# A planned instruction order, and the recurrent state brought back through DVE squares and DRAM, in a four-layer graph network on one core

## The chip, the core and the metric

The kernel runs on one core of a Trainium2 chip. The metric is the time of one execution on the device, in microseconds (us); less is better. Each ratio below compares a kernel with the kernel before, run on the same chip, one after the other. The experiments ran on three chips, and on each the kernel before came out within 0.6 us of the others in its median, so medians are compared across them too.

Engines: PE is TensorE (matmuls and transposes), PEld its weight loads, DVE the vector engine, ACT the scalar engine, POOL GpSimd, SP the engine that issues most of the DMAs here. PE multiplies a stationary operand (the weights, 128x128) with a moving one (up to 512 columns).

## The reference, cut to what matters

```python
x: (32, 512, 128)   adj: (512, 512)          # 32 batches of 512 tokens with 128 features
x = x + gcn(relu(layernorm(x)))              # A_norm @ h @ W.T + b
x = x + ggnn(relu(layernorm(x)))             # five recurrent steps, below
x = x + elu(gat(relu(layernorm(x))))         # attention over the edges
x = x + gat(relu(layernorm(x)))

def step(h):                                 # of ggnn, five times
    m = adj @ h
    av = concat([m, m])
    u3 = h @ u3_w.T + u3_b
    z = sigmoid(av @ w3_w.T + w3_b + u3)
    r = sigmoid(av @ w4_w.T + w4_b + u3)
    hv = tanh(av @ w5_w.T + w5_b + (r * h) @ u5_w.T + u5_b)
    return (1 - z) * h + z * hv
```

All of it is float32. The batches are independent, the five steps of a batch are not.

## The kernel before

In a step, `adj @ h` needs the state with tokens on the partitions (`h`, it is the stationary operand), everything after it needs the features on the partitions (`hT`). Four batches ("lanes") are in flight, one step apart, so that PE always has another batch's work. After each step PE transposes the new `hT` back:

```python
def product(p, h, mT):
    for c in range(C):                                        # C = 4 chunks of 128 tokens
        nc.tensor.matmul(flat(p), h[:, c, :], mT[:, c, :], start=(c == 0), stop=(c == C - 1))

def ggnn_reset(b, s):
    ...
    nc.tensor.matmul(flat(p), wT["w4"], m, start=True, stop=False)
    nc.tensor.matmul(flat(p), wT["u3"], hT, start=False, stop=True)
    nc.scalar.activation(r, flat(p), AF.Tanh, bias=gate_b["w4"], scale=0.5)
    nc.vector.scalar_tensor_tensor(rh, r, 1.0, hT, op0=ALU.add, op1=ALU.mult)

def ggnn_update(b, s):
    ...                                                       # z the same way with w3
    nc.tensor.matmul(flat(q), wT["w5"], m, start=True, stop=False)
    nc.tensor.matmul(flat(q), wT["u5"], rh, start=False, stop=True)     # PE needs rh here
    nc.scalar.activation(hv, flat(q), AF.Tanh, bias=gate_b["w5"])
    ...                                                       # three DVE operations make the new hT

def ggnn_back(b, s):
    p = bank("back")
    to_features(p, hT.rearrange("p (c k) -> p c k", c=C))     # four PE transposes
    if s < STEPS - 1:
        h = work.tile([P, C, D], F32, name="h", bufs=LANES + 3)
        nc.scalar.copy(flat(h), flat(p))
    else:
        nc.vector.scalar_tensor_tensor(flat(xs[b]), flat(xs[b]), -1.0, flat(p), ...)

def gat_edges(b, l):                                          # four of these stand on DVE per layer
    for j in range(C):
        nc.vector.scalar_tensor_tensor(e[:, j, :], flat(row), h[:, j, D + 1:D + 2], maskT[l][:, j, :],
                                       op0=ALU.max, op1=ALU.mult)

def wide():                                                   # one double PSUM bank for all GAT layers
    return psum.tile([P, C, 2 * P], F32, name="wide")
```

The functions are called in a fixed pattern of turns. From that the framework's own scheduler makes the order in which each engine takes its instructions.

The softmax here doesn't subtract the row's maximum and nothing guards it: scores larger than these inputs give would overflow.

Of the kernel before, what the change touches and what calls it, by code (L numbers as in the profile page):

```python
# [16 lines left out]
SLOPE = 0.2  # L17
LANES = 4


@with_exitstack
def gnn_stack(ctx: ExitStack, tc: tile.TileContext, a: dict, out: bass.AP):
# [5 lines left out]
    const = ctx.enter_context(tc.tile_pool(name="const", bufs=1))  # L28
    state = ctx.enter_context(tc.tile_pool(name="state", bufs=1))
    stat = ctx.enter_context(tc.tile_pool(name="stat", bufs=4))  # L30

    psum = ctx.enter_context(tc.tile_pool(name="psum", bufs=1, space=bass.MemoryType.PSUM))

    def bank(name, bufs=1):
        return psum.tile([P, C, P], F32, name=name, bufs=bufs)

    def side_bank():
        return bank("side", 2)

    def wide():  # L40
        return psum.tile([P, C, 2 * P], F32, name="wide")
# [3 lines left out]


    setup = ctx.enter_context(ExitStack())
    raw = setup.enter_context(tc.tile_pool(name="raw", bufs=1))
    adj_sb = raw.tile([P, C, N], F32, name="adj_sb")
    for c in range(C):  # L50
        nc.sync.dma_start(adj_sb[:, c, :], adj[c * P:(c + 1) * P, :])

    def load(pool, name, shape, src):
        t = pool.tile(shape, F32, name=name)
        nc.scalar.dma_start(t, src)
        return t

    def column(v):
        return v if len(v.shape) == 2 else v.rearrange("(p o) -> p o", o=1)

    w0 = load(raw, "w0", [P, D], a["L0_gnn_W"])
    b0 = load(const, "b0", [P, D], bass.AP(tensor=a["L0_gnn_b"].tensor, offset=a["L0_gnn_b"].offset,
                                           ap=[[0, P], [1, D]]))
    w1 = {k: load(raw, k, [P, a["L1_gnn_" + k + "_w"].shape[1]], a["L1_gnn_" + k + "_w"])
          for k in ("w3", "u3", "w4", "w5", "u5")}
    b1 = {k: load(raw, "b" + k, [P, 1], column(a["L1_gnn_" + k + "_b"]))
          for k in ("w3", "u3", "w4", "w5", "u5")}
    gat_w = {2: a["L2_gnn_W"], 3: a["L3_gnn_w"]}
    w_aug, a_pair = {}, {}
    for l in (2, 3):  # L70
        w_aug[l] = const.tile([P, D + 3], F32, name=f"w_aug{l}")
        nc.scalar.dma_start(w_aug[l][:, :D], gat_w[l])
        a_pair[l] = raw.tile([P, 2], F32, name=f"a_pair{l}")
        nc.scalar.dma_start(a_pair[l][:, 0:1], column(a[f"L{l}_gnn_a_src"]))
        nc.scalar.dma_start(a_pair[l][:, 1:2], column(a[f"L{l}_gnn_a_dst"]))

    xs = []
    for b in range(B):
        t = state.tile([P, C, D], F32, name=f"x{b}")
        nc.sync.dma_start(t, x[b].rearrange("(c p) d -> p c d", p=P))  # L80
        xs.append(t)


    ident = const.tile([P, P], F32, name="ident")
    make_identity(nc, ident)
    mhalf = const.tile([P, C], F32, name="mhalf")
    nc.gpsimd.memset(mhalf, -0.5)

    adjT = const.tile([P, C, N], F32, name="adjT")
    for m in range(C):  # L90
        p = side_bank()
        for c in range(C):
            nc.tensor.transpose(p[:, c, :], adj_sb[:, c, m * P:(m + 1) * P], ident)
        nc.scalar.copy(adjT[:, m, :], flat(p))
    deg = raw.tile([P, C], F32, name="deg")
    nc.vector.reduce_sum(deg, adj_sb, axis=mybir.AxisListType.X)
    nc.vector.tensor_scalar_add(deg, deg, 1.0)
    dinv = raw.tile([P, C], F32, name="dinv")
    nc.gpsimd.tensor_tensor(dinv, deg, mhalf, ALU.pow)


    anT = const.tile([P, C, N], F32, name="anT")
    nc.vector.tensor_copy(anT, adjT)
    for c in range(C):
        blk = anT[:, c, c * P:(c + 1) * P]
        nc.vector.tensor_add(blk, blk, ident)
    drow = side_bank()
    for c in range(C):
        nc.tensor.transpose(drow[:, c, :], dinv[:, c:c + 1].to_broadcast([P, P]), ident)
    maskT = {l: const.tile([P, C, N], BF16, name=f"maskT{l}") for l in (2, 3)}  # L110
    nc.vector.tensor_scalar(maskT[2], anT, 0.0, None, op0=ALU.is_gt)
    for m in range(C):
        nc.vector.scalar_tensor_tensor(anT[:, m, :], anT[:, m, :], dinv[:, m:m + 1], flat(drow),
                                       op0=ALU.mult, op1=ALU.mult)
    nc.vector.tensor_scalar(maskT[3], adjT, 0.0, None, op0=ALU.is_gt)

    def transposed(name, w, scale=None):
        p = side_bank()
        nc.tensor.transpose(p[:, 0, :], w, ident)
        t = const.tile([P, P], F32, name=name)  # L120
        if scale is None:
            nc.scalar.copy(t, p[:, 0, :])
        else:
            nc.scalar.mul(t, p[:, 0, :], scale)
        return t

    w0T = transposed("w0T", w0)


    ws = {}  # L130
    for k in ("w3", "w4", "w5"):
        ws[k] = raw.tile([P, D], F32, name=k + "s")
        nc.vector.tensor_add(ws[k], w1[k][:, :D], w1[k][:, D:])
    nc.vector.tensor_sub(ws["w3"], ws["w3"], ws["w4"])
    wT = {k: transposed(k + "T", ws[k]) for k in ("w4", "w3", "w5")}
    wT["u3"] = transposed("u3T", w1["u3"])
    wT["u5"] = transposed("u5T", w1["u5"], 0.5)
    gate_b = {}
    for k, u, half in (("w3", "u3", True), ("w4", "u3", True), ("w5", "u5", False)):
        gate_b[k] = const.tile([P, 1], F32, name="gate_b" + k)  # L140
        nc.vector.tensor_add(gate_b[k], b1[k], b1[u])
        if half:
            nc.vector.tensor_scalar_mul(gate_b[k], gate_b[k], 0.5)


    for l in (2, 3):
        gT = transposed(f"gat_wT{l}", w_aug[l][:, :D])
        a3 = raw.tile([P, 3], F32, name=f"a3_{l}")
        nc.vector.tensor_scalar_mul(a3[:, 0:1], a_pair[l][:, 1:2], SLOPE)
        nc.vector.tensor_scalar_mul(a3[:, 1:2], a_pair[l][:, 1:2], 1.0 - SLOPE)  # L150
        nc.vector.tensor_scalar_mul(a3[:, 2:3], a_pair[l][:, 0:1], SLOPE - 1.0)
        p = side_bank()
        nc.tensor.matmul(p[:, 0, :3], gT, a3, start=True, stop=True)
        nc.vector.tensor_copy(w_aug[l][:, D:D + 3], p[:, 0, 0:3])

    setup.close()
    work = ctx.enter_context(tc.tile_pool(name="work", bufs=2))


    def norm_stats(b):  # L160
        st = stat.tile([P, C, 6], F32, name="st")
        mv = stat.tile([P, C, 2], F32, name="mv")
        for c in range(C):
            nc.vector.bn_stats(st[:, c, :], xs[b][:, c, :])  # L164
        for c in range(C):
            nc.vector.bn_aggr(mv[:, c, :], st[:, c, :])
        ve = stat.tile([P, C], F32, name="ve")
        nc.vector.tensor_scalar_add(ve, mv[:, :, 1], EPS)
        rstd = stat.tile([P, C], F32, name="rstd", bufs=8)
        nc.gpsimd.tensor_tensor(rstd, ve, mhalf, ALU.pow)  # L170
        return mv, rstd

    def norm_relu(b, y):

        mv, rstd = norm_stats(b)
        off = stat.tile([P, C], F32, name="off")
        nc.vector.scalar_tensor_tensor(off, mv[:, :, 0], -1.0, rstd, op0=ALU.mult, op1=ALU.mult)
        for c in range(C):
            nc.scalar.activation(y[:, c, :], xs[b][:, c, :], AF.Relu, bias=off[:, c:c + 1],  # L179
                                 scale=rstd[:, c:c + 1])  # L180

    def to_features(p, y):
        for c in range(C):
            nc.tensor.transpose(p[:, c, :], y[:, c, :], ident)  # L184

    def product(p, h, mT):

        for c in range(C):
            nc.tensor.matmul(flat(p), h[:, c, :], mT[:, c, :], start=(c == 0), stop=(c == C - 1))  # L189

    kept = {}


    def gcn_in(b):
        y = work.tile([P, C, D], F32, name="y", bufs=3)
        norm_relu(b, y)
        nc.gpsimd.tensor_tensor(xs[b], xs[b], b0[:, None, :].to_broadcast([P, C, D]), ALU.add)
        kept["y", b] = y

    def gcn_prod(b):  # L200
        p = side_bank()
        product(p, kept.pop(("y", b)), anT)
        m = work.tile([P, N], F32, name="m0")
        nc.scalar.copy(m, flat(p))
        kept["m0", b] = m

    def gcn_out(b):
        m = kept.pop(("m0", b))
        p = side_bank()
        for c in range(C):  # L210
            nc.tensor.matmul(p[:, c, :], m[:, c * P:(c + 1) * P], w0T, start=True, stop=True)  # L211
        nc.vector.tensor_add(flat(xs[b]), flat(xs[b]), flat(p))
# [144 lines left out]
    for t in range(first, last + 1):  # L357
# [3 lines left out]
        for k, f in side:  # L361
            b, rest = divmod(t - k, STEPS)
            if rest == 0 and 0 <= b < B:
                f(b)
# [30 lines left out]
```

## Time and profile before

| | before |
|---|---|
| time, median of 3 runs | 1883.92 us (1883.11 to 1884.14) |
| span of the profiled run | 1882.5 us |
| PE busy, its share of the chain that ended last | 97%, 96% |
| DVE busy, ACT busy | 55%, 38% |
| first product of the first GCN starts at | 29.95 us |

The prediction shows the lines of this profile that matter and says how to read them. A matmul's own duration is not its price, since matmuls overlap; the price is the distance from its start to the start of the next. A dense PE starts a 512-column record every 0.4285 us (a float32 matmul is two such records), a 129- or 131-column one every 0.112 us and a transpose every 0.109 us. Sum these over all records and you have the PE work; what a stretch of the trace is longer than its work is time that PE lost, by waiting or by a slower clock. For this kernel that gives:

| | before the first record | PE work | lost to 60 us | lost 60 to 1690 us | lost from 1690 us | after the last start | sum = span |
|---|---|---|---|---|---|---|---|
| before | 3.8 | 1801.2 | 34.6 | 5.6 | 32.6 | 4.8 | 1882.5 |

The middle is dense; what is to be had lies in the work itself, and at the two ends.

### The profile page before, as it was taken

What the parts mean: (1) busy time and instruction counts of PE and PEld (TensorE: products, weight loads), DVE (VectorE), ACT (ScalarE), POOL (GpSimd) and SP (SyncE); (2) the same over time, 40 slices, a digit from 0 to 9 for tenths busy, and PEclk for the clock granted to TensorE, in tenths of its full rate; (3) what the DMA queues carried; (4) which work ended last, traced back from release to release, by engine and by line L of the source; (5) the groups of instructions that cost most, each with busy time, mean ns of one, the idle gap of its engine ahead of it and who ended that gap; (6) DMA issues with size and microseconds to landing.
All of it is one profiled execution on the core that took longest, in us unless ns stands there. A gap on an engine that the chain in (4) does not pass through costs nothing.

```text
span 1882.5 us, 19768 instructions
## 1 busy us (share of the span) xinstructions
PE 1832.7 (97%) x7264; PEld 1052.9 (56%) x7264; DVE 1039.3 (55%) x2814; ACT 723.8 (38%) x1453; POOL 184.7 (10%) x168
## 2 busy tenths in 40 slices
PE   4999999999999999999999999999999999999995
PEld 2444556555556555556555556555555555555664
DVE  3334565555565555555565556565556565555665
ACT  2444443443343444343444344344344344333321
POOL 1101010110010111011111011111011011000000
PEclk9999999999999999999999999999999999999997
DMA  8000000000000000000000000000000000000000
GB/s 218 1 1 1 0 6 7 6 1 6 6 6 7 6 1 6 6 6 7 6 1 6 6 6 6 6 1 6 7 6 7 6 1 6 6 6 6 6 12 12
DMA packets 37056, 19.88 MB, mean 11 GB/s; under 512 B 2528, under 2 KB 36448, under 8 KB 36960
## 3 DMA queue, kind: packets, MB, share of 16 engines
q1 hardware_dynamic: 34368, 17.83, 3.3%
q8 instruction: 57, 0.93, 0.2%
q10 hardware_dynamic: 2592, 0.79, 0.2%
q14 instruction: 39, 0.32, 0.1%
HBM read 10.23 MB, written 8.39 MB: 10 GB/s over the span
## 4 chain that ended last, share of the span: by engine, by line
PE 96%; DVE 2%; DMA 1%; ACT 1%; issue 0%; POOL 0%; SPq 0%; ACTq 0%; DVEq 0%; POOLq 0%
PE prod L189 29%; PE wide L323 12%; PE gate L247 7%; PE cand L252 7%; PE gate L237 7%; PE cand L251 7%; PE gate L238 7%; PE side L189 6%; PE back L184 4%; PE wide L296 3%; PE side L184 2%; PE side L211 2%; PE side L311 1%; DMA x<-in_x_dram 1%; DMA u<-in_L_gnn_u_w_dram 0%
## 5 line engine op out<-in xcount | busy, mean ns | idle before, releaser
L189 PE MATMUL prod<-adjT,h 128*128 128x512 f32 x1280 | 583.2, 594 | 0.0
L189 PEld LDWEIGHTS prod<-adjT,h 128*128 128x128 f32 x1280 | 240.4, 191 | 285.7 <-issue 285.6
L255 DVE TENSOR_TENSOR hv<-hv,hT 128x512 f32<-128x512 f32 x160 | 111.0, 694 | 481.8 <-ACT hv L254 481.8
L170 POOL TENSOR_TENSOR rstd<-ve,mhalf 128x4 f32<-128x4 f32 x128 | 129.4, 1011 | 1557.4 <-DVE off L282 973.0
L323 PEld LDWEIGHTS wide<-h_gat,e 128*128 128x128 f32 x2048 | 238.3, 193 | 20.5 <-issue 11.6
L323 PE MATMUL wide<-h_gat,e 128*128 128x129 f32 x2048 | 241.8, 276 | 3.5 <-DVE o L338 1.5
L231 ACT COPY m<-prod 128x512 f32<-128x512 f32 x160 | 93.1, 582 | 328.6 <-PE prod L189 328.6
L240 ACT ACTIVATE r<-gate,gate_bw 128x512 f32<-128x512 f32 x160 | 109.9, 687 | 277.4 <-PE gate L238 273.6
L314 DVE SCALAR_TENSOR_TENSOR e<-side,h_gat,maskT 128x512 f32<-128x512 f32 x256 | 183.6, 741 | 4.2 <-PE side L311 4.0
L242 DVE SCALAR_TENSOR_TENSOR rh<-r,hT 128x512 f32<-128x512 f32 x160 | 109.4, 684 | 106.2 <-ACT r L240 106.0
L237 PE MATMUL gate<-m,w4T 128*128 128x512 f32 x320 | 164.2, 595 | 2.0 <-ACT m L231 1.5
L247 PE MATMUL gate<-m,w3T 128*128 128x512 f32 x320 | 164.3, 595 | 0.2 <-ACT r L240 0.2
L252 PE MATMUL cand<-rh,u5T 128*128 128x512 f32 x320 | 163.5, 592 | 0.3 <-DVE rh L242 0.3
L238 PE MATMUL gate<-hT,u3T 128*128 128x512 f32 x320 | 163.4, 592 | 0.0
L251 PE MATMUL cand<-m,w5T 128*128 128x512 f32 x320 | 163.4, 592 | 0.0
L254 ACT ACTIVATE hv<-cand,gate_bw 128x512 f32<-128x512 f32 x160 | 109.1, 682 | 97.2 <-PE cand L252 96.8
L258 DVE SCALAR_TENSOR_TENSOR hT<-hv,hT 128x512 f32<-128x512 f32 x160 | 134.7, 842 | 2.6 <-DVE arg L298 0.2
L184 PEld LDWEIGHTS back<-ident,hT 128*128 128x128 f32 x640 | 79.8, 141 | 84.8 <-issue 81.9
L285 ACT ACTIVATE y<-x,off 128x128 f32<-128x128 f32 x256 | 87.7, 393 | 92.7 <-DVE off L282 92.7
L249 ACT ACTIVATE z<-gate,gate_bw 128x512 f32<-128x512 f32 x160 | 109.5, 684 | 27.9 <-PE gate L247 27.9
L164 DVE BATCH_NORM_STATS2 st<-x 128x6 f32<-128x128 f32 x512 | 119.0, 280 | 1.2
L189 PE MATMUL side<-anT,y 128*128 128x512 f32 x256 | 117.4, 601 | 1.9 <-ACT y L179 1.9
(93 smaller groups left out, 1625.8 us busy)
## 6 DMA issues: line engine op xcount, KB each, us to landing
x<-in_x_dram SPq DMA_DIRECT2D x32, 256.0 KB, 5.4
out_dram<-o SPq DMA_DIRECT2D x32, 256.0 KB, 2.2
adj_sb<-in_adj_dram SPq DMA_DIRECT2D x4, 256.0 KB, 5.3
w<-in_L_gnn_w_w_dram ACTq DMA_DIRECT2D x3, 128.0 KB, 5.6
u<-in_L_gnn_u_w_dram ACTq DMA_DIRECT2D x2, 64.0 KB, 4.5
w<-in_L_gnn_W_dram ACTq DMA_DIRECT2D x1, 64.0 KB, 3.0
b<-in_L_gnn_b_dram ACTq DMA_DIRECT2D x1, 64.0 KB, 5.4
w_aug<-in_L_gnn_W_dram ACTq DMA_DIRECT2D x1, 64.0 KB, 3.7
```

The source lines that it names most:

```text
L164: nc.vector.bn_stats(st[:, c, :], xs[b][:, c, :])
L170: nc.gpsimd.tensor_tensor(rstd, ve, mhalf, ALU.pow)
L184: nc.tensor.transpose(p[:, c, :], y[:, c, :], ident)
L189: nc.tensor.matmul(flat(p), h[:, c, :], mT[:, c, :], start=(c == 0), stop=(c == C - 1))
L237: nc.tensor.matmul(flat(p), wT["w4"], m, start=True, stop=False)
L238: nc.tensor.matmul(flat(p), wT["u3"], hT, start=False, stop=True)
L247: nc.tensor.matmul(flat(p), wT["w3"], m, start=False, stop=True, skip_group_check=True)
L251: nc.tensor.matmul(flat(q), wT["w5"], m, start=True, stop=False)
L252: nc.tensor.matmul(flat(q), wT["u5"], rh, start=False, stop=True)
L258: nc.vector.scalar_tensor_tensor(new, hv, 0.5, hT, op0=ALU.mult, op1=ALU.add)
L314: nc.vector.scalar_tensor_tensor(e[:, j, :], flat(row), h[:, j, D + 1:D + 2], maskT[l][:, j, :], op0=ALU.max, op1=ALU.mult)
L323: nc.tensor.matmul(p[:, c, :D + 1], e[:, j, c * P:(c + 1) * P], h[:, j, :D + 1], start=(j == 0), stop=(j == C - 1))
```

## The change

Its intent: take 640 transposes off PE, the engine that bounds, and give them to DVE and to DMA, which have room; and fix the order of every engine from a plan, so that the longer way back is behind other work.

The order first. Each piece of work is entered with its engine, an assumed duration and a due time; a small event simulation in the kernel starts on each engine whatever is ready and due first, and the instructions are then emitted in that order, which the framework leaves alone:

```diff
+    def op(self, engine, cost, due, emit, r=(), w=(), delay=None):
+        ...                                     # dependencies from what is read and written
+    def run(self):
+        ...                                     # list scheduling with the costs and delays below
+        self.order, self.end = order, now
+        for o in order:
+            o.emit()
...
+    MM, MM1, TURN = 0.86, 0.235, 0.117          # us that the plan assumes on PE
+    V, A = 0.61, 0.62                           # and on DVE and ACT for 128x512
...
+    with tc.manual_schedule():
+        plan.run()
```

Then the way back. DVE transposes 32x32 squares; four DMAs write the squares to DRAM, where they fall into place, and one reads the state back with tokens on the partitions. In `h` the four chunks lie interleaved, so that a chunk is read as weights with a step of four floats:

```diff
-        p = bank("back")
-        to_features(p, hT.rearrange("p (c k) -> p c k", c=C))
-        if s < STEPS - 1:
-            h = work.tile([P, C, D], F32, name="h", bufs=LANES + 3)
-            nc.scalar.copy(flat(h), flat(p))
+        form = "p q (c j) -> p q c j" if last else "p q (j c) -> p q c j"
+        op("DVE", 0.61 if last else 1.0, due - 5, lambda: nc.vector.transpose(
+            sq.t.rearrange(form, c=C), flat(new.t).rearrange("p (c q i) -> p q c i", c=C, q=Q)), r=[new], w=[sq])
+        for k in range(Q):
+            op("SP", 0.44, due, lambda k=k: nc.sync.dma_start(
+                far.t[:, :, k, :].rearrange("q i f -> i q f"), sq.t[k * W:(k + 1) * W]), r=[sq], w=[far[k]], delay=1.7)
+        op("SP", 0.4, due, lambda: nc.sync.dma_start(h.t, far.t.rearrange("q i k f -> (q i) k f")),
+           r=[far], w=[h], delay=2.5)
...
+    def chunk(h, c):
+        return h.t.rearrange("p k (j c) -> p c (k j)", c=C)[:, c, :]
```

Beside these, the loads move from ACT to SP, the masks and biases stand elsewhere in the order, and a constant is folded into a bias. The rest of the diff is the old kernel written in the new form.

## The prediction

> **What bounds the kernel now.** I read first the busy shares and the slices of the page, then the chain that ended last, then the groups of PE, then one stretch of PE's timeline, then busy times in windows.
>
> ```profile
> PE 1832.7 (97%) x7264; PEld 1052.9 (56%) x7264; DVE 1039.3 (55%) x2814; ACT 723.8 (38%) x1453; POOL 184.7 (10%) x168
> ...
> PEclk9999999999999999999999999999999999999997
> ...
> PE 96%; DVE 2%; DMA 1%; ACT 1%; issue 0%; POOL 0%; SPq 0%; ACTq 0%; DVEq 0%; POOLq 0%
> ...
> L189 PEld LDWEIGHTS prod<-adjT,h 128*128 128x128 f32 x1280 | 240.4, 191 | 285.7 <-issue 285.6
> ...
> out_dram<-o SPq DMA_DIRECT2D x32, 256.0 KB, 2.2
> ```
>
> PE is busy 97% of the span and carries 96% of the chain: TensorE is the bound, DVE and ACT have much room. What one piece of PE work costs is not its mean duration (matmuls overlap) but the distance between starts:
>
> ```profile
> 214.08 3.60 PE L189 MATMUL prod<-adjT,h 128*128 128x512 f32 x8
> 217.52 0.60 PE L184 MATMUL back<-ident,hT 128*128 128x128 f32 x4
> 217.95 1.02 PE L247 MATMUL gate<-m,w3T 128*128 128x512 f32 x2
> 218.81 1.02 PE L251 MATMUL cand<-m,w5T 128*128 128x512 f32 x2
> ```
>
> A 128x512 f32 matmul (two records) takes 0.86 us, the four transposes of "back" 217.95-217.52 = 0.43 us; the 16 matmuls of L323 run from 208.79 to 212.37, 0.224 us each. A batch comes to: 5 steps x (9x0.857 + 0.437) = 40.8; GCN 4x0.857 + 4x0.224 = 4.3; first turn 0.44; two GATs x (0.437 + 0.89 + 0.437 + 3.58) = 10.7; together 56.2. The trace repeats every 56.27 us (L323 starts at 208.96, 265.23, 321.49 in the chain), so the middle is dense to 0.2%. 32x56.27 = 1801, so some 82 us of the 1882.5 are lost at the ends. The windows show it:
>
> ```profile
> 0.00:20.00 20.00, 5.45 (x20) 3.83 (x21) 6.09 (x28) 3.53 (x5) 2.78 (x9) 1.00 0.79 227
> 20.00:40.00 20.00, 11.27 (x30) 5.41 (x28) 9.63 (x26) 4.38 (x13) 2.04 (x2) 0.99 1.13 285
> ...
> 100.00:400.00 300.00, 300.00 (x1082) 162.41 (x1081) 154.99 (x422) 125.03 (x246) 31.20 (x27) 1.00 0.01 3
> ...
> 1800.00:1850.00 50.00, 40.84 (x208) 28.16 (x206) 32.84 (x94) 14.19 (x33) 4.05 (x4) 0.90 0.03 8
> 1850.00:1870.00 20.00, 11.34 (x77) 10.08 (x78) 9.24 (x28) 2.12 (x6) 1.01 (x1) 0.81 0.05 14
> ```
>
> After the window's length comes PE busy; the third number from the right is the granted clock, the last two the DMA share and GB/s. In the first 100 us the matmuls counted there are worth 55.7 us at the dense pace, so 44 us are lost (setup included); after 1800 us they are worth 47 of 82.5, so 35 us are lost.
>
> **What the Trainium skill says.** "TensorE: Matmul & The Clock Gate", Part 4, gives a transpose about 275 ns in a kernel; the trace has 274 ns for "back", but its price here is the 0.109 us between starts. The same page, Part 1, says that the array falls to half rate after an idle window; the trace agrees: the last L323 group, after idle time, takes 6.28 us for the work that takes 3.58 when dense. "VectorE: DVE Perf Modes", The three transpose paths: DVE transposes 32x32 blocks only, hence the trip through DRAM to place the blocks; it gives the clock as 0.96 GHz. The kernel before has no such transpose to compare. "Advanced Engine Details and Errata", SBUF Cachelines: a different 16-byte line per access is penalized; the new h is read as weights with a step of 4 floats, exactly one line per element. No run of before shows what that costs.
>
> **The change, part by part.**
>
> 1. Removed: 640 transposes on PE, 160 groups x 0.437 = 70 us, all on the bound. Nothing else of PE's work changes (the instruction order of the changed kernel has the same 1568 wide matmuls, 1024+256+128 narrow ones and 640 remaining transposes of 128 columns). 128 copies of h on ACT go too (75.7 us); ACT is not the bound, worth 0.
>
> 2. Added on DVE: 160 square transposes of 128x512. At one element per cycle (my estimate, with that clock) 533 ns; L255 of the same size takes 694 ns, and writing with a step of 16 bytes may cost more, so I estimate 0.8 to 1.0 us, 130 to 160 us in all. DVE 1039 + 145 = 1185 us, 66% of the new span: beside PE, not on the path. Added DMA: 5 per step. The one-line cost of issuing the output is 0.37 us and its landing 2.2 us, so a trip is 3x0.37 + 2.2 (four writes) + 0.1 + 2.2 (the read, which must wait for the landings) = 5.6 us.
>
> 3. Is the trip hidden? From the trace a step alone: product start to m ready 4.2 (1797.09 to 1801.32); two matmuls and tanh to 7.0; rh to 7.7; u5 and tanh to 9.5; three DVE operations of 0.72 to 11.7; then square 0.9 and trip 5.6: 18.3 us. Before, the return was 0.4 + 0.2 + 0.6. With four lanes in flight, the other three lanes alone give PE 3x7.7 = 23 us, and a step's turn in the steady state is four slots of 54.1/5 = 10.8, 43 us. Hidden in the middle; worth 0 there. The period should fall from 56.27 to 56.27-2.19 = 54.1.
>
> 4. Start. Before, ACT issues 18 loads before it copies adjT, and the first GCN product starts at 29.95. Now ACT issues two and SP the rest; in the new DVE order anT still stands behind the adjacency, and the first y behind the biases, and ACT's first y behind the last GAT weights: 21 loads on SP, 12 us of issue (0.95 for an x, about 0.4 for a small one, as before) plus a landing of about 3, plus 2 for transposes, copies and y: 17.5 us. After it six GCNs stand back to back on PE before the first lane, so the ramp should be nearly dense: 1.7 for the cold clock, 2.5 for small gaps.
>
> 5. End. In the new PE order the last batch runs its steps 1 to 4 with few others beside it: in the last three of them no other lane is left. From the first of these products on (73.5 us of PE work at the dense pace remain) the end is a chain: 4 steps x 18.3 + 0.7 for the addition to x = 74 us, then two GATs in series. In the trace the last GAT pair takes from 1837.5 to 1882.5 with another batch between; the lone parts are 1862.95 to 1882.5 = 19.6 for the second, about 20 for the first: 40. So 114 us for 73.5 us of work: 40 us lost, where before lost 35. Here the trip is exposed four times (4 x 5 = 20 us); the order takes part of it back with GAT work.
>
> Sum: 17.5 + 1.7 + 2.5 + PE work between the first GCN product and the last chain (counted from the order: 1655) + stalls in the middle, 0.5% = 8, + 114 = **1799 us** span. The timed runs lie 1.4 us above the span of before: **1800 us**, 0.955 of before. In other words: -70 for the transposes, -22 at the start, +5 at the end, +4 more stalls in the middle.
>
> **The rivals.**
>
> A. The order is worth nothing, only the transposes leave: 1884-70 = 1814. For it: the middle was already dense. Against: the first 30 us are visibly wasted. Near enough to be in the range.
>
> B. Strided weights. 1280 loads of h, 191 ns each, are issued 0.43 us apart, with 0.24 us of slack ("idle before", ended by issue). Doubled to 0.38 they still hide. If they went to 0.55, each record would lose 0.12, 154 us in all, and the kernel would be slower than before, some 1950. I give it 4%.
>
> C. The fixed order waits. Engines take instructions in program order, and a plan made with assumed durations may place a product before its h has landed. If every step lost 0.5 us, +80: 1875; the slack of 43 against 18 us speaks against it, but the planner also sets gates only two matmuls (1.7 us) behind the product whose copy (1.0 us after the product's end) they need, so small stalls are likely. I carry 8 us, and up to 30 in the range.
>
> D. DVE becomes the bound: needs 1800, has about 1200. Locally, where a GAT's edges (2.7 us) stand ahead of rh, a wait of a us or so may reach PE; that is in C.
>
> E. DMA bandwidth: 512 KB per step are 82 MB, 46 GB/s on average, against 227 to 285 GB/s in the first windows. Not a bound.
>
> **Range and chances.** Start uncertain by 4, end by 10, middle by -6 to +25: **1778 to 1828**. Only B, or C at three times its upper size, reaches 1846 (2% faster). Faster 0.94, within 2% 0.04, slower 0.02.
>
> **What would show it.** Right: no "back" row on PE and PE's busy time lower by about 70; L518 groups of one layer 54 us apart; weight loads of h between 190 and 400 ns with PE still dense in 300 us windows; first GCN product near 17.5; DVE square at 0.8 to 1.0; the trip 5 to 6.5 us; in the last 115 us PE busy for about 75. Wrong: PE idle before products waiting on the DMA of h in the middle (C), or start-to-start of the product's records over 0.43 (B), or a tail of well over 115 us.

## The result

| | median | runs | span of the profiled run |
|---|---|---|---|
| before | 1883.51 us | 4 (1882.41 to 1884.14) | 1882.5 us |
| after | 1816.34 us | 4 (1815.74 to 1817.36) | 1814.0 us |

The ratio is 0.9645, with a 95% interval of 0.9628 to 0.9661. A ratio here is the mean time of one kernel's fast runs over that of the other's in the same rounds, so it isn't quite the ratio of the medians. The predicted time was 1800 us with a range of 1778 to 1828: the kernel is faster, inside the range, and 16 us above its centre.

From the page of the changed kernel: engines busy, the granted PE clock in 40 slices, the chain that ended last, and two groups with their count, total busy time and mean duration in ns, then the idle time before them.

```profile
PE 1773.6 (98%) x6624; PEld 1143.2 (63%) x6624; DVE 1189.3 (66%) x2981; ACT 672.5 (37%) x1322; POOL 180.4 (10%) x168
...
PEclk9999999999999999999999999999999999999999
...
PE 94%; DVE 3%; DMA 1%; issue 0%; POOL 0%; ACT 0%; SPq 0%; DVEq 0%; POOLq 0%; ACTq 0%
...
L397 PEld LDWEIGHTS bank<-adjT,h 128*128 128x128 f32 x1280 | 385.7, 311 | 144.7 <-issue 36.0
...
L463 DVE STREAM_TRANSPOSE sq<-hT 128x512 f32<-128x512 f32 x160 | 164.7, 1029 | 4.4 <-DMA far<-sq 1.8
...
far<-sq SPq DMA_DIRECT2D x640, 64.0 KB, 1.8
h<-far SPq DMA_DIRECT2D x160, 256.0 KB, 2.6
```

PE has 640 instructions fewer and is still the bound. The load of the strided weights takes 311 ns where the load of contiguous ones took 191. The new DVE squares take 1.03 us on average: 1.11 us for the 128 that write with a step of 16 bytes, 0.71 us for the 32 of the last steps, which don't. The last column of the DMA rows is the median from issue to landing: 1.8 us for each write and 2.6 us for the read back.

The same stretches as before, and two more (after the length come PE, PEld, DVE, ACT and POOL busy with their counts, then the clock, the DMA share and GB/s):

```profile
0.00:20.00 20.00, 10.56 (x35) 7.45 (x36) 14.50 (x62) 7.39 (x16) 6.09 (x11) 1.00 0.76 223
20.00:40.00 20.00, 19.15 (x59) 9.46 (x58) 18.50 (x97) 10.94 (x27) 15.03 (x13) 1.00 0.97 289
100.00:400.00 300.00, 299.38 (x926) 179.75 (x925) 182.07 (x409) 118.52 (x218) 24.45 (x22) 1.00 0.22 57
...
1750.00:1790.00 40.00, 28.41 (x187) 25.57 (x188) 29.42 (x88) 8.81 (x26) 4.10 (x5) 0.87 0.08 20
1790.00:1814.00 24.00, 12.37 (x88) 11.08 (x86) 10.35 (x25) 0.43 (x2) 0.00 (x0) 0.89 0.11 34
```

The start is far denser, and the end is as empty as it was. The 299.38 of the middle window hides what matters there: matmuls that start late still overlap each other, so PE counts as busy. The distances between starts show it:

| | before the first record | PE work | lost to 60 us | lost 60 to 1690 us | lost from 1690 us | after the last start | sum = span |
|---|---|---|---|---|---|---|---|
| before | 3.8 | 1801.2 | 34.6 | 5.6 | 32.6 | 4.8 | 1882.5 |
| after | 4.4 | 1731.4 | 15.7 | 22.7 | 34.9 | 4.9 | 1814.0 |

So 69.8 us of work left, 18.9 us were won at the start, and 17.1 us were lost in the middle, where the prediction had 4 more than before. Where do they arise? One stretch of PE's timeline in the changed kernel (start, length, instruction, count):

```profile
1725.06 1.16 PE L495 MATMUL wide<-w_aug,gT 128*128 128x131 f32 x8 [0.42 <-DVE gT L490]
1726.06 3.71 PE L397 MATMUL bank<-adjT,h 128*128 128x512 f32 x8
1729.61 0.60 PE L508 MATMUL bank<-ident,h_gat 128*128 128x128 f32 x4
```

The product takes 1729.61 - 1726.06 = 3.55 us for eight records that are worth 3.43. It follows narrow matmuls. Between 17 us and 1700.8 us (the start of the last chain of the prediction), products of `h` that follow narrow matmuls or transposes lost 16.8 us in 124 places, 0.135 us each; products that follow wide matmuls lost 0.008 us each. The few such places in the kernel before lost 0.006 us each.

### The profile page after: what moved, and what is told of

Its sections match the earlier page's. It is cut to its first block, busy times and chain, and to the rows that moved or that the text cites. A ratio compares the mean times of both kernels' runs of the same rounds, so it can differ in the third digit from the quotient of the medians.

```text
span 1814.0 us, 20223 instructions
## 1 busy us (share of the span) xinstructions
PE 1773.6 (98%) x6624; PEld 1143.2 (63%) x6624; DVE 1189.3 (66%) x2981; ACT 672.5 (37%) x1322; POOL 180.4 (10%) x168
## 3 DMA queue, kind: packets, MB, share of 16 engines
q1 hardware_dynamic: 151872, 102.04, 21.3%
## 4 chain that ended last, share of the span: by engine, by line
PE 94%; DVE 3%; DMA 1%; issue 0%; POOL 0%; ACT 0%; SPq 0%; DVEq 0%; POOLq 0%; ACTq 0%
PE bank L397 36%; PE wide L518 13%; PE bank L441 8%; PE cand L448 8%; PE cand L449 8%; PE bank L434 8%; PE bank L435 7%; PE wide L495 3%; PE bank L389 2%; PE bank L508 1%; PE bank L413 1%; DVE e L511 1%; DVE st L356 1%; DMA h<-far 0%; DVE off L370 0%
## 5 line engine op out<-in xcount | busy, mean ns | idle before, releaser
L397 PE MATMUL bank<-adjT,h 128*128 128x512 f32 x1280 | 611.5, 605 | 0.6 <-DMA h<-far 0.6
L397 PEld LDWEIGHTS bank<-adjT,h 128*128 128x128 f32 x1280 | 385.7, 311 | 144.7 <-issue 36.0
L518 PEld LDWEIGHTS wide<-h_gat,e 128*128 128x128 f32 x2048 | 247.2, 195 | 47.0 <-issue 27.5
L518 PE MATMUL wide<-h_gat,e 128*128 128x129 f32 x2048 | 250.1, 279 | 11.2 <-DVE h_gat L502 4.1
L399 ACT COPY m<-bank 128x512 f32<-128x512 f32 x192 | 112.1, 584 | 280.9 <-PE bank L397 280.0
L511 DVE SCALAR_TENSOR_TENSOR e<-bank,h_gat,maskT 128x512 f32<-128x512 f32 x256 | 175.2, 738 | 13.7 <-PE bank L508 13.4
L463 DVE STREAM_TRANSPOSE sq<-hT 128x512 f32<-128x512 f32 x160 | 164.7, 1029 | 4.4 <-DMA far<-sq 1.8
L441 PE MATMUL bank<-m,wT 128*128 128x512 f32 x320 | 163.9, 594 | 1.7 <-ACT r L437 1.7
L434 PE MATMUL bank<-m,wT 128*128 128x512 f32 x320 | 163.8, 593 | 1.4 <-ACT m L399 1.4
L448 PE MATMUL cand<-m,wT 128*128 128x512 f32 x320 | 163.5, 592 | 0.0
L449 PE MATMUL cand<-rh,wT 128*128 128x512 f32 x320 | 163.5, 592 | 0.0
L435 PE MATMUL bank<-hT,wT 128*128 128x512 f32 x320 | 163.4, 592 | 0.0
L397 PE MATMUL bank<-anT,y 128*128 128x512 f32 x256 | 122.8, 607 | 1.6 <-DVE x L415 0.9
```

The source lines that it names most:

```text
L397: op("PE", MM, due, lambda c=c: nc.tensor.matmul(flat(p.t), chunk(h, c), mT.t[:, c, :], start=(c == 0), stop=(c == C - 1)), r=[h[c] if len ...
L399: op("ACT", A, due, lambda: nc.scalar.copy(flat(m.t), flat(p.t)), r=[p], w=[m])
L434: nc.tensor.matmul(flat(gate.t), gates.t[:, 0, :], flat(m.t), start=True, stop=False)
L435: nc.tensor.matmul(flat(gate.t), gates.t[:, 1, :], flat(hT.t), start=False, stop=True)
L441: op("PE", MM, due + 0.3, lambda: nc.tensor.matmul(flat(gate.t), gates.t[:, 2, :], flat(m.t), start=False, stop=True, skip_group_check=Tru ...
L448: nc.tensor.matmul(flat(cand.t), gates.t[:, 3, :], flat(m.t), start=True, stop=False)
```

## The experiments

Eleven kernels ran, all with three rounds but the one with a step of two, which had a single look. All are judged by the same table, which stands at the end of this section. The kernel before was run beside them, with medians of 1883.15, 1883.15 and 1882.92 us over 7 runs each.

### The strided weights

The theory: a 512-column record of 0.43 us covers a weight load of 311 ns, a narrow one of 0.11 us does not, so the first loads of a product after narrow work stand open. The edit reads each chunk contiguously from the same tile. Its output is wrong, which doesn't matter for the time. Every instruction and its place stay.

```diff
-        return h.t.rearrange("p k (j c) -> p c (k j)", c=C)[:, c, :]
+        return h.t.rearrange("p k f -> p (k f)")[:, c * P:(c + 1) * P]
```

> The changed kernel with one edit: the weights of the product over h are read as 128 floats in a row instead of with a step of 4 floats (the values are then wrong, on purpose; instructions, order and transfers are the same). Theory S (the middle lost 16.8 us because a strided weight load of 0.31 us cannot hide behind a narrow matmul): weight loads of h back at about 0.19 us, no extra gap where a product follows a narrow group, 1799 us (1795 to 1803). Rival C (the fixed order waits for data): loads faster, but the time stays at 1816, give or take 3.

Measured: 1801.20 us (1801.19 to 1801.48), ratio 0.9564 (0.9549 to 0.9578); relative error 0.637.

```profile
L397 PEld LDWEIGHTS bank<-adjT,h 128*128 128x128 f32 x1280 | 233.4, 190 | 248.3 <-issue 241.4
```

The load is back at 190 ns and the time falls by 15.1 us; in the middle PE loses 8.3 us where it lost 22.7. The strided weights are worth nearly as much as the 16 us between the prediction and the result.

A second kernel used a step of two floats, with wrong values again.

> Wrong values on purpose: the weights of the product are read with a step of two floats (8 bytes) instead of four (16 bytes), two of them in each 16-byte line; nothing else changes. If the load pays by the 16-byte lines that it touches (32 lines 190 ns, 128 lines 311 ns): some 230 ns for 64 lines. If any step but one costs the same: 311 ns. If two elements to a line already hide it: 190 ns. Time: between 1801 and 1816 in the first case.

Measured: one run, 1802.17 us, of unknown state; relative error 0.649.

```profile
L397 PEld LDWEIGHTS bank<-adjT,h 128*128 128x128 f32 x1280 | 241.4, 196 | 243.1 <-issue 236.9
```

196 ns: the third guess holds. A step of 8 bytes costs almost nothing, a step of 16 bytes 120 ns. The Trainium skill says this in "Advanced Engine Details and Errata", SBUF Cachelines, in a sentence that the prediction passed over: "Need at least two hits on a cacheline to absorb SRAM access latency". These two runs agree with it.

### A correct kernel with contiguous weights

The read back from DRAM puts each chunk in its place, in four DMAs with runs of 128 bytes, and the square is written with unit steps.

```diff
-        op("SP", 0.4, due, lambda: nc.sync.dma_start(h.t, far.t.rearrange("q i k f -> (q i) k f")),
-           r=[far], w=[h], delay=2.5)
+            for c in range(C):
+                op("SP", 0.4, due, lambda c=c: nc.sync.dma_start(
+                    h.t[:, c, :].rearrange("p (k j) -> p k j", k=Q),
+                    far.t.rearrange("q i k (c j) -> (q i) k c j", c=C)[:, :, c, :]),
+                   r=[far], w=[h] if c == 0 else [h[c]], delay=2.5)
```

> Correct version of the contiguous weights: the read of the trip puts h down chunk by chunk, in runs of 128 bytes (four reads instead of one), so that the weights of the product are contiguous, and the DVE square uses the form with unit steps. Theory S (the strided weights behind narrow matmuls cost what the run with contiguous weights gained, and the longer read hides in the middle): weight load of h 190 ns, DVE square 0.69 us, median 1801 (1796 to 1808). Rival (the read now has 2048 runs of 128 bytes a step; estimated from the DMA share of the changed kernel, where about 950 packets a step take 21% of 16 engines, some 2600 packets take 58%, and the reads land 8 us or later): products then wait on the DMA of h also in the middle, 1816 or more.

Measured: 1805.06 us (1804.08 to 1805.60), ratio 0.9583 (0.9568 to 0.9597), correct.

```profile
q1 hardware_dynamic: 403776, 102.06, 26.7%
...
L463 DVE STREAM_TRANSPOSE sq<-hT 128x512 f32<-128x512 f32 x160 | 112.9, 706 | 2.6
...
h<-far SPq DMA_DIRECT2D x512, 64.0 KB, 2.4
```

The q1 row is the DMA queue: packets, megabytes, and the share of the 16 DMA engines. It has 403776 packets instead of 151872, but its share only grows from 21.3 to 26.7%, where I had estimated 58%, and a quarter of the state lands 2.4 us after its issue. The rival's short packets are a small burden here: the time is 3.9 us above that of the contiguous weights with wrong values (in the middle 11.1 us are lost against 8.3), and 11.3 us are won with correct values. The square falls to 706 ns; what that is worth by itself, no run shows.

### The order alone

The planned order, with PE transposes and the ACT copy in the place of the trip:

```diff
+        p = Val("bank")
+        op("PE", C * TURN, due + 0.5, turns, r=[new, ident], w=[p])
+        ...
+        op("ACT", A, due, lambda: nc.scalar.copy(flat(h.t), flat(p.t)), r=[p], w=[h])
```

> The planned order kept, the trip undone: every step's state goes back to tokens by four PE transposes and an ACT copy into a contiguous h. Theory (the trip is worth its transposes, less strided loads, less its exposure in the tail): 1816 + 70 for 640 transposes - 17 for strided loads - 21 for four exposed trips of 5.3 us = 1848 us (1840 to 1856), so the order alone is worth some 36 us. Rival O (the planned order is worth only the start, 22 us): 1862 or more.

Measured: 1868.64 us (1868.01 to 1869.62), ratio 0.9922 (0.9907 to 0.9936), correct. I was wrong here and the rival right. The order wins 19.5 us in the first 60 us (34.6 lost before, 15.1 now), gives 3.0 back in the middle and leaves the end as it was (32.1 against 32.6). That the end didn't shrink without any trip also says that the exposed trips were not what the end cost. One thing isn't separated: "the order" here holds all that the new kernel does otherwise, so also the loads that moved from ACT to SP. The gain lies at the start, where ACT had issued 18 loads before its first copy of `adjT`, and the moved loads may be worth most of it.

### The trip alone

The old kernel with the old scheduler's order, and in `ggnn_back` the DVE square and the DRAM trip.

```diff
-        p = bank("back")
-        to_features(p, hT.rearrange("p (c k) -> p c k", c=C))
+        nc.vector.transpose(sq.rearrange(form, c=C), hT.rearrange("p (c q i) -> p q c i", c=C, q=Q))
+        for k in range(Q):
+            nc.sync.dma_start(far[:, :, k, :].rearrange("q i f -> i q f"), sq[k * W:(k + 1) * W])
+        nc.sync.dma_start(h, far.rearrange("q i k f -> (q i) k f"))
```

> The kernel before, in its own order, with only ggnn_back replaced by the DVE square and the DRAM trip (and h read with a step of 4 floats, -1 folded into the bias). Theory (the trip is hidden in the middle with four lanes in either order): 1884 - 70 for the transposes + 15 to 20 for exposed trips in the tail = 1832 us (1820 to 1845); PE dense from 100 to 1700. Rival W (only a planned order hides the trip): products wait on the DMA of h in the middle, 1850 us or more.

Measured: 1882.82 us (1881.89 to 1883.28), ratio 0.9997 (0.9981 to 1.0014), correct. The 70 us of work are gone and nothing is won. Both of my theories fail: the waits aren't on the trip. What PE waited for (total us, times, longest), the first row and the row for the trip:

```profile
PE cand L264 <- DVE rh L254: 27.0, 26, 1.1
...
PE prod L199 <- DMA h<-far: 4.4, 1, 4.4
```

26 waits, and they come every 55.5 us: once per batch. One of them, from the timeline:

```profile
700.28 0.67 ACT L252 ACTIVATE r<-gate,gate_bw 128x512 f32<-128x512 f32 x1
...
701.89 0.74 DVE L332 SCALAR_TENSOR_TENSOR e<-side,h_gat,maskT 128x512 f32<-128x512 f32 x1
...
702.56 0.68 DVE L322 TENSOR_TENSOR h_gat<-wide,k 128x512 f32<-128x512 f32 x1
...
703.15 1.39 DVE L332 SCALAR_TENSOR_TENSOR e<-side,h_gat,maskT 128x512 f32<-128x512 f32 x2
704.47 0.68 DVE L254 SCALAR_TENSOR_TENSOR rh<-r,hT 128x512 f32<-128x512 f32 x1
...
705.20 1.13 PE L264 MATMUL cand<-rh,u5T 128*128 128x512 f32 x2 [1.08 <-DVE rh L254]
```

`r` is ready at 700.95. `rh` needs only `r` and `hT`, but in DVE's queue it stands behind an `e`, an `h_gat` and two more `e` of the attention layers, and begins at 704.47. PE stands still for 1.08 us. It can't take other matmuls meanwhile: the Trainium skill, "TensorE: Matmul & The Clock Gate", Part 2, says that matmuls stay in program order and only weight loads are pulled ahead, and the trace agrees (the next matmuls of PE's order start only after this one). The kernel before has the same queue, and there `rh` is some 3 us late in 25 places too; PE comes to the `u5` matmul late enough not to notice (0.3 us of waits in all). As far as the two traces tell, the work that was taken off PE had covered a delay on DVE.

The test: give `rh` and the three state updates priority.

```diff
-        nc.vector.scalar_tensor_tensor(rh, r, 1.0, hT, op0=ALU.add, op1=ALU.mult)
+        with tc.high_priority():
+            nc.vector.scalar_tensor_tensor(rh, r, 1.0, hT, op0=ALU.add, op1=ALU.mult)
```

(And the three state updates the same way.)

> The trip alone in the old order (1882.8, no gain), with rh and the three state updates given priority on the vector engine. In the trip alone, 24 of the 25 waits of the candidate matmul in the middle have one and the same picture: rh stands behind one h_gat and three e of the attention layers, 4 us late, 1.23 us of TensorE each, 30 us in all; the new order puts exactly this rh ahead of them and leaves the matmul order almost untouched. Theory (vector queue order gave the gain back): these waits go, 1883 - 30 = 1853 (1846 to 1862). Rival (the wait only moves, to the attention matmuls that need the e now later, or to the attention mix): 1870 or more.

Measured: 1849.96 us (1849.61 to 1852.24), ratio 0.9824 (0.9810 to 0.9839), correct. PE's own order is the same but for a few lines. The loss in the middle falls from 60.0 to 25.6 us, and of the 27.0 us that PE waited for `rh` 0.3 us in one place are left. That was the cause of these waits: one DVE instruction per batch, in the wrong place of a queue. (The three state updates were moved with it; no run moves `rh` alone.) What still separates this kernel from the changed one (34 us) is the start (34.0 lost against 15.7) and the end (48.2 against 34.9), with 2.9 in the middle. In the old order the trip also costs at the end: 46.7 us are lost there in the trip alone, 32.6 in the kernel before. None of PE's waits there is on the read back; what grew is its wait for `gT`, a copy on DVE, from 0.8 to 7.0 us. Why, the runs don't show.

### Is the trip hidden, and by what?

The prediction said that it is hidden by slack: 43 us for a turn, 18 for a step. To test the slack, one more hop from DRAM to DRAM makes each trip some 3 us longer, behind the plan's back: the order of every engine stays.

```diff
+    def hop(far, h):
+        t = far2[next(turn2) % 4]
+        nc.sync.dma_start(t.rearrange("q i k f -> (q i) k f"), far.t.rearrange("q i k f -> (q i) k f"))
+        nc.sync.dma_start(h.t, t.rearrange("q i k f -> (q i) k f"))
```

> One more hop from DRAM to DRAM in every trip, about 2.5 us longer, the order of all engines unchanged and planned without it. Theory (the trip is hidden in the middle with more than 2.5 us to spare, exposed at most in the last steps): 1816 to 1824. Rival (the plan has set each product just behind the landing that it assumed, so each of the 128 trips between steps that is longer by 2.5 us shows on TensorE): 128 x 2.5 / (four lanes in flight) = 80 us or more, 1896 or more.

Measured: 1976.09 us (1970.02 to 1978.44), ratio 1.0481 (1.0459 to 1.0502), correct. My theory falls by 150 us. The first row of PE's waits:

```profile
PE bank L397 <- DMA h<-far_b: 64.6, 29, 5.8
```

One of the 29 places on PE's timeline, 2.25 us of waiting before the product, and then 5.52 us for eight records:

```profile
332.53 5.52 PE L397 MATMUL bank<-adjT,h 128*128 128x512 f32 x8 [2.25 <-DMA h<-far_b]
```

Within the product nothing is waited for: its first four records start 0.85 us apart and the last ones 0.43, and the trace grants half the clock for 3.4 us from 333.0 on. So a wait is paid twice here. The same stretch in the changed kernel and in this one (the third number from the right is the clock):

```profile
60.00:1690.00 1630.00, 1628.64 (x5977) 1042.36 (x5976) 1061.68 (x2523) 614.75 (x1192) 139.82 (x125) 1.00 0.21 54
...
60.00:1690.00 1630.00, 1541.54 (x5456) 959.68 (x5456) 968.40 (x2312) 563.08 (x1092) 133.68 (x118) 0.97 0.27 72
```

PE loses 163.6 us in the middle, 141 more than in the changed kernel. Its waits in this stretch come to 88 us, 61 of them on the read back and the others on ACT and DVE, which wait in their turn. The clock cost some 34 us: 142 records start at about double their dense distance. I then matched, in the changed kernel's trace, each read back with the product that uses it: of the 128 products, 41 start less than 3 us after their state has landed, and the median is 7.3 us. (The landing is the issue plus the 2.6 us of the DMA row. The match needs the batch of each record, which comes from running the kernel's own plan.) What these 41 lack to 3 us is 65 us together, about what PE then waited for the read back. The plan always takes the batch that is due first, and that batch runs as fast as its chain allows. The slack of 43 against 18 us exists, but the order spends it, and an order, once fixed, can't wait for anything without waiting for all of it.

Then the plan should also be able to hide the longer trip, if it is told:

```diff
+        op("SP", 0.5, due, lambda: nc.sync.dma_start(
+            far2.t.rearrange("q i k f -> (q i) k f"), far.t.rearrange("q i k f -> (q i) k f")), r=[far], w=[far2], delay=2.7)
+        op("SP", 0.4, due, lambda: nc.sync.dma_start(h.t, far2.t.rearrange("q i k f -> (q i) k f")),
+           r=[far2], w=[h], delay=2.5)
```

> The same longer trip (one hop more from DRAM to DRAM, 2.9 us to land), but this time entered in the plan as an instruction of its own with its landing time, so that the order of all engines is made for it. Theory P (the trip is hidden because the plan knows how long it is, not because products stand far behind their landings): the middle is dense again and only the last steps pay, by the plan's own arithmetic 16 us more at the end than the changed kernel: 1832 (1822 to 1842). Rival (the longer trips are too much for the one queue or for the four lanes, whatever the order): 1880 or more, as in the unplanned run's 1976.

Measured: 1834.39 us (1833.07 to 1836.98), ratio 0.9740 (0.9723 to 0.9756), correct. From the end of the square to the landing, the median trip takes 9.1 us, in the unplanned run 9.0, in the changed kernel 5.8. The same longer trip costs 160 us in an order that doesn't know it and 18 us in one that does, and those lie in the end (53.7 lost against 34.9). One thing differs beside the order: in the unplanned run SP waits for the hop with the next trip's DMAs behind it. The lengths of the trips, nearly equal at the median, 11.2 and 10.5 us at the ninetieth percentile, suggest that this is the smaller part; the runs don't separate it further. In the planned run even more products, 51 of 128, start less than 3 us after their landing, yet the middle loses only 24.1 us: little slack is harmless while the durations are as planned.

### The end

First suspicion: the exposed trips. The last batch's steps 1 to 4 go back by PE transposes.

```diff
+        if b == B - 1 and s > 0:
+            ...                                  # four PE transposes and a copy, as in the order alone
```

> The changed kernel, but the last batch returns its steps 1 to 4 by PE transposes and a copy (correct values). Theory T (in the tail the end is a chain of four lone steps, each with an exposed square and trip): 4 x (1.0 + 5.5 - 1.2) = 21 us less, 1795 us (1788 to 1803). Rival: the tail is set by the GATs and the PE work left over, so 1811 or more.

Measured: 1816.94 us (1816.26 to 1818.29), ratio 0.9648 (0.9633 to 0.9662), correct. The last state is there 63.6 us ahead of the end instead of 55.1, and nothing is won. So what follows it sets the end. In the changed kernel:

```profile
1792.38 1.16 PE L495 MATMUL wide<-w_aug,gT 128*128 128x131 f32 x8 [0.85 <-DVE h_gat L502]
...
1798.84 5.27 PE L518 MATMUL wide<-h_gat,e 128*128 128x129 f32 x32 [3.72 <-DVE h_gat L502]
1805.55 3.84 PE L518 MATMUL wide<-h_gat,e 128*128 128x129 f32 x32 [1.44 <-DVE x L535]
```

Both attention products (L518) and the heads (L495) write `wide`, the one double bank. The first L518 waits until DVE has read the other batch's heads out of it (`h_gat`), the second until DVE has read the first. Two things beside the bank lengthen this. In DVE's order that `h_gat` stands behind five `e`, four of them of the later batch (0.67 us each):

```profile
1794.82 3.37 DVE L511 SCALAR_TENSOR_TENSOR e<-bank,h_gat,maskT 128x512 f32<-128x512 f32 x5
1798.11 0.68 DVE L502 TENSOR_TENSOR h_gat<-wide,k 128x512 f32<-128x512 f32 x1
```

A better place in that queue is a rival to more banks, and no run tests it. And after the wait 13 records start 0.215 us apart before the pace of 0.112 is back, 1.3 us. The edit gives the last two batches two single banks instead (chunks 0 and 1 in one, 2 and 3 in the other), of which five are in the pool:

```diff
-        q, arg, k = Val("wide"), Val("arg"), Val("k")
+        split = 2 if b >= B - 2 else 1
+        qs = [Val("bank") for _ in range(2)] if split == 2 else [Val("wide")]
...
-        p, rden = Val("wide", C), Val("rden")
+        ps = [Val("bank", per) for _ in range(2)] if split == 2 else [Val("wide", C)]
```

> The changed kernel, but the last two batches' attention layers use two single banks instead of the one double bank that all attention layers share. Theory (at the end the two batches' attention layers queue on the one double bank): the end 5 to 8 us earlier, 1808 to 1811. Rival (the vector engine, about 0.9 busy there, is the limit, and more but smaller vector instructions make it no better): 1814 or more.

Measured: 1808.63 us (1806.46 to 1809.18), ratio 0.9600 (0.9586 to 0.9614), correct. The end loses 28.5 us instead of 34.9, and nothing else moves. The last mixes now run without a break:

```profile
1795.80 6.82 PE L531 MATMUL bank<-h_gat,e 128*128 128x129 f32 x56
```

### All of it at once

Contiguous `h` by an ACT copy after the trip, PE transposes for steps 1 to 4 (but the last) of the last two batches, single banks for the attention of the last four, and masks and gate biases behind the scaled adjacency at the start.

```diff
-        return h.t.rearrange("p k (j c) -> p c (k j)", c=C)[:, c, :]
+        return h.t[:, c, :]
...
+        op("ACT", A, due, lambda: nc.scalar.copy(
+            h.t.rearrange("p c (k j) -> p k c j", k=Q), back.t.rearrange("p k (c j) -> p k c j", c=C)), r=[back], w=[h])
```

> Everything that the runs point to at once, correct values: h laid out contiguously by a copy on the scalar engine after the trip (weights without a step, DVE square with unit steps), the last two batches' steps 1 to 4 but the last back by TensorE transposes, the last four batches' attention layers in two single banks, and at the start the masks and gate biases behind the scaled adjacency on the vector engine. Sum of the parts: 1816.3 - 15 (weights) - 10 (end, the difference that the plan itself gives) - 2 (start) = 1789 (1784 to 1798). Rival (160 more copies on the scalar engine, 0.6 to 0.9 us each and in its fixed order, hold up tanh and the copies of m, which TensorE then waits for): 1800 or more.

Measured: 1786.35 us (1785.71 to 1787.15), ratio 0.9485 (0.9470 to 0.9499), correct. It beats both kernels.

```profile
PE 1755.3 (98%) x6648; PEld 988.9 (55%) x6648; DVE 1140.1 (64%) x3003; ACT 738.5 (41%) x1450; POOL 181.0 (10%) x168
...
L399 PEld LDWEIGHTS bank<-adjT,h 128*128 128x128 f32 x1280 | 233.5, 190 | 246.2 <-issue 240.0
```

These two are from its page; from the groups by line comes the row of the new copies, with what ended the idle time before them:

```profile
L479 ACT COPY h<-back 128x512 f32<-128x512 f32 x122 | 74.8, 613 | 60.7 <-DMA back<-far 60.0
```

The copies take 74.8 us of ACT beside PE, and no loss in the middle shows that PE pays for them. The middle loses 5.5 us, as before the change, and the end 20.7. The start didn't gain: the first GCN product starts at 15.9 instead of 17.0 us, but the first 60 us lose as much as they did.

All kernels, in us of the profiled run:

| kernel | PE work | lost to 60 us | lost 60 to 1690 us | lost from 1690 us | span |
|---|---|---|---|---|---|
| before | 1801.2 | 34.6 | 5.6 | 32.6 | 1882.5 |
| after | 1731.4 | 15.7 | 22.7 | 34.9 | 1814.0 |
| contiguous weights, wrong values | 1731.4 | 14.9 | 8.3 | 35.4 | 1799.7 |
| step of two, wrong values | 1731.5 | 14.4 | 9.8 | 34.9 | 1800.4 |
| contiguous by DMA | 1731.5 | 14.9 | 11.1 | 37.0 | 1803.8 |
| order alone | 1801.2 | 15.1 | 8.6 | 32.1 | 1866.4 |
| trip alone | 1731.5 | 33.2 | 60.0 | 46.7 | 1880.1 |
| trip alone, rh first | 1731.4 | 34.0 | 25.6 | 48.2 | 1848.1 |
| longer trip, not planned | 1731.4 | 15.1 | 163.6 | 56.8 | 1976.6 |
| longer trip, planned | 1731.4 | 15.0 | 24.1 | 53.7 | 1833.8 |
| PE transposes at the end | 1733.2 | 15.2 | 22.1 | 34.5 | 1814.9 |
| single banks at the end | 1731.4 | 15.4 | 22.5 | 28.5 | 1807.0 |
| all at once | 1734.1 | 15.6 | 5.5 | 20.7 | 1785.3 |

The rest of each span, 8.5 to 10.0 us, lies before the first PE record and after the start of the last.

## Why the prediction was right or wrong

**The total** was 16 us too low, inside the range. By its own sum: start 17.5 (measured 17.0), ramp 1.7 + 2.5 (6.5), work 1655 (1654.7), middle stalls 8 (22.6), last chain 114 (113.2). The total alone proves little: rival A, "the order is worth nothing", said 1814 and lies nearer to the measured 1816.3 than the 1800 does. Only the parts decide.

**Step 1, the removed transposes,** was right in size: 69.8 us of PE work left against 70. That they are worth their full size isn't a matter of course. The trip without the planned order wins nothing, the order (with the moved loads) without the trip 15 us, both together 67. Some 33 of the remaining 52 us are the one late `rh` per batch (1882.8 against 1850.0 us); in the changed kernel PE's waits show none for `rh`.

**Step 2, DVE and the trip:** squares predicted at 0.8 to 1.0 us and measured at 1.11 with the step (1.03 over all), DVE 1185 us and 1189.3, a trip 5.6 us and 5.8 at the median.

**Step 3, "hidden in the middle; worth 0 there",** was right in its result: PE waited for the read back for 0.6 us in all. Its reason was wrong. It compared 43 us of turn with 18 us of step, but in the changed kernel's trace a third of the products have less than 3 us to spare, and the longer trip shows what that means. The trip is hidden because the plan assumes nearly the landing times that the chip has (1.7 and 2.5 us assumed, 1.8 and 2.6 measured).

**The middle stalls, 8 us,** are the term that was mis-sized, and they are the error of the whole. They measured 22.6 us, of which 16.8 stand at products after narrow matmuls. (What is left with contiguous weights, 8.3 us, is near the 8 that it carried for rival C.) The prediction put strided weights (rival B) down as all or nothing: hidden in the slack of 0.24 us, or 154 us lost. It let loads of up to 0.38 us hide; they took 0.311 and didn't. The slack of 0.24 us holds between two wide records, but at 124 places the first load of a product stands behind a narrow one. The runs with contiguous weights and with a step of two floats show that the step is the cause. That it works by loads which a narrow matmul is too short to cover is argued, not shown. The difference fits (311 - 190 = 121 ns, 0.135 us lost per place), but by that account alone a contiguous load of 190 ns behind a record of 112 ns would lose 0.08 us too, and at these places it loses about 0.01.

**Step 4, the start,** was right: 17.0 us against 17.5. Rival A, that the order is worth nothing, falls: without the trip it is worth 15 us, with the loads that moved.

**Step 5, the end,** was right only in its sum, and that was luck. It had four lone steps of 18.3 us, 74 with the addition, and two attention layers of 40. By the kernel's plan the products of the last chain are steps 3 and 4 of batches 30 and 31 in turn (two of them start 12.2 us apart in the trace, less than a lone step), so the steps are over after 58 us, and the attention layers that are left, of batches 29 to 31, then take 55, one behind the other on one double bank. The trip was named as exposed four times there, at 20 us; taking it away for the last batch won nothing.

**Rivals C, D and E:** stalls by the fixed order were large only where the chip didn't keep the plan's durations (the unplanned longer trip). DVE and DMA bandwidth bound nothing. D did name the place, an `rh` behind a GAT's edges, and put it at a us or so: in the old order that wait, once per batch, cost the trip alone some 33 us, by DVE's queue and not its load.

**Two readings** of the profile before were off, without weight in the sum. By the starts, 40.8 us are lost in the first 100 us, not 44. And the 6.28 us of the last L323 group are not the half clock alone: its first seven records start 0.28 to 0.38 us apart because they wait for `e`; the half clock shows in the nine after them, 0.215 us apart, before the pace falls to 0.112.

## What to carry to other kernels

When work leaves the bounding engine, look for what that work had been covering: here an instruction late in another engine's queue, which had cost nothing until then. A fixed order hides a latency only as far as it was planned with it, so measure the durations that a plan assumes, and expect its slack to be used up. A wait of PE can cost twice, since the clock that the trace grants was halved after it. Weights whose load is hidden behind wide matmuls must still be asked what they follow when the matmul before them is narrow.

## What the Trainium skill lacked or had wrong

- "Advanced Engine Details and Errata", SBUF Cachelines, has the rule (two hits on a line absorb the latency) but no size and no word on weight loads. For a load of 128x128 f32: 190 ns contiguous, 196 ns with a step of 8 bytes, 311 ns with a step of 16. It cost 0.135 us where a product followed narrow matmuls, and nothing of note behind 512-column ones.
- "VectorE: DVE Perf Modes", The three transpose paths, gives 311 ns for a 128x128 bf16 transpose and nothing for f32 or for a strided output. A 128x512 f32 transpose took 706 ns with unit steps, and 1109 ns with an output step of 16 bytes.
- "DMA: Bandwidth & Descriptors", Specifications, puts the smallest transfer for line rate at 512 bytes. Here runs of 128 bytes into SBUF raised the share of the DMA engines only from 21.3 to 26.7% for 2.7 times the packets, and 64 KB landed in 2.4 us. At 58 GB/s on average this says nothing about line rate, and so nothing against the page; in this kernel, far below it, they cost some 4 us of 1805.
